# Where the last block's ssm residual stands between two ff groups, and three smaller placements, in a conditioned block kernel on Trainium2

## The chip, the cores and the metric

The kernel runs on one core of one Trainium2 chip. The metric is the device time of one execution in microseconds (us). A core has TensorE (PE; PEld is its weight load), VectorE (DVE), ScalarE (ACT), GpSimd (POOL), and SyncE (SP), which here only issues DMAs. Each engine takes its own instructions in the order in which the program issued them, and waits on semaphores for the others.

## The reference

Two sequences of 2048 tokens with 512 features pass one conditioned block. `cond` gives six modulation vectors for each sequence.

```python
emb = jnp.dot(jax.nn.silu(t), ada_w) + ada_b
shift_msa, scale_msa, gate_msa, shift_mlp, scale_mlp, gate_mlp = jnp.split(emb, 6, axis=-1)
norm = _ln(x) * (1.0 + scale_msa[:, None]) + shift_msa[:, None]
h = jax.nn.gelu(jnp.dot(norm, ssm_w1) + ssm_b1, approximate=False)
ssm_out = jnp.dot(h, ssm_w2) + ssm_b2
x = x + gate_msa[:, None] * ssm_out
norm2 = _ln(x) * (1.0 + scale_mlp[:, None]) + shift_mlp[:, None]
hf = jax.nn.gelu(jnp.dot(norm2, ff_w1) + ff_b1, approximate=True)
ff_out = jnp.dot(hf, ff_w2) + ff_b2
x = x + gate_mlp[:, None] * ff_out
```

The ssm weights are 512 x 512, ff_w1 is 512 x 1024, ff_w2 is 1024 x 512. All is fp32.

## The kernel before

**Tiles.** The 4096 tokens are eight blocks of 512 (`NBLK` = 8, four for each sequence). A block's tile `x_i` is 128 partitions x 4 x 512. All weights stay in SBUF. Each 512 x 512 product of a block is done by Strassen's method in Winograd's form: seven half-size products P1 to P7 instead of eight, with sums of quarters of both operands made ahead (`sums_of_first`, `sums_of_second`: four operations in order, which also overwrite one quarter).

**Groups.** `group` (L268) issues the seven products in the order P1, P2, P6, P5, P7, P3, P4 (in the start also FIRST, with P5 ahead of P6). A product has two halves j, and each half 2 or 4 values of k. Products accumulate in three PSUM banks: P1, P6, P7 and P4 in "y", P2 in "x", P5 and P3 in "v". Each tag has two buffers, one for each group in turn. After each product `after` reads the bank (VectorE, in P4 of hidden groups ScalarE), and then the operations hung on that product in `hooks` are issued. So the place of a hook is its place in the queues of all engines. `EARLY` is P1, P2, P6, P5, P7.

**Stages of a block i.** Names in the profile follow them:
- `hA_i`: first ssm product and gelu (`First`); `hSA` are the sums of its result.
- `oA_i`: second ssm product, added to x_i (`residual`, L469, read at L483).
- `hC_i`: first ff product, in two groups of 256 hidden columns each, `hC_i_0` and `hC_i_1` (`Second`); `hSC` are the sums of its result, `hC.summed(0)` and `hC.summed(1)`.
- `oC_i`: second ff product, added to x_i, then stored.

A norm (`Norm`) consists of `stats` (VectorE), `scales` (eight small POOL instructions, L325 to L336), `normal` (ScalarE, L349), `turn` (VectorE, 32 x 32 transposes), `move` (sixteen DMAs on SP that exchange blocks between partitions, L369), `moved` (ScalarE, modulation, L392) and `summed` (L218 to L221). In the start, `normal` is followed by TensorE transposes instead (`turned`, L378).

**The main loop (L700)**, for block i: hC_i group 0, hC_i group 1, oA_{i+1}, oC_i, hA_{i+2}. In group 1, n1 of block i+2 is scaled, normalized, turned and moved; in oA_{i+1} it is modulated, and at P3 and P4 the stats of n2 of block i+1 are taken. In oC_i that norm is scaled, normalized (P1), turned (P2, P2, P6), moved (P6) and modulated (P3), and after oC_i its sums are made on POOL. Blocks 6 and 7 have no hA_{i+2}; after oC_6, hC_7 follows at once. In the last oC_7 only P4 is `parted`: each half is read and stored for itself.

**The start.** `IDLE` = 6 matmuls on the identity come first. SP issues the loads of x_0, ada_0, ada_1, w1, ada_2, w2, x_1, ada_3, ada_4, b2's row (`b2_bc`), fw1, later ada_5 and fw2. In hA_0, `ssm_gate` multiplies b2's row with the gate (L630), folds the gate into w2 (L251, `fold2`: four folds on VectorE and four sums on POOL), and the four biases (L496) follow on POOL. Operation 7 of `fold2` is the last sum, L221. `n1[1].scales` opens the hooks of oA_0.

Of the kernel before, what the change touches and what calls it, by code (L numbers as in the profile page):

```python
# [36 lines left out]
F32 = mybir.dt.float32  # L37
# [6 lines left out]
def kernel(  # L44
# [17 lines left out]
    P = 128  # L62
# [23 lines left out]
    out_blk = out.flatten_outer_dims().rearrange("(i p c) d -> i p c d", p=P, c=C)  # L86

    G = 32
    IDLE = 6


    R_COND, R_ADA = 0, B * KD
# [8 lines left out]
    def load_x(i, pieces=1):  # L101
        xs[i] = big_tile(f"x_{i}")
        for s in range(pieces):
            c = slice(s * C // pieces, (s + 1) * C // pieces)
            nc.sync.dma_start(out=xs[i][:, c, :], in_=x_blk[i][:, c, :])
# [3 lines left out]
    def load_ada(g):  # L109
        ada[g] = big_tile(f"ada_{g}")  # L110
        nc.sync.dma_start(
            out=ada[g], in_=ada_w[:, g * D : (g + 1) * D].rearrange("(k p) n -> p k n", p=P)
        )
# [7 lines left out]
    def load_row(t, row):  # L121
        nc.sync.dma_start(out=t, in_=row.unsqueeze(0).to_broadcast([P, D]))
        return t
# [21 lines left out]
        )  # L145
    w2_sb = load_w("w2", w2)
    load_x(1)
    load_ada(3)
    load_ada(4)
    b2_bc = work.tile([P, D], F32, tag="gb", name="gb2_0", bufs=2)  # L150
    load_row(b2_bc, b2)
    fw1_sb = load_w("fw1", fw1)

    def ada_rows(g, bias=None, pa=None):
# [113 lines left out]
    def group(name, kdim, lhs, rhs, after, hooks, parted=(), order=ORDER):  # L268


        ps = {}
        for p in order:
            b = BANK[p]
            fresh = b not in ps
            if fresh:
                ps[b] = ps_g.tile([P, 2, HT], F32, tag=b, name=f"p{b}_{name}")
            for j in range(2):
                for k in range(kdim):
                    nc.tensor.matmul(  # L279
                        ps[b][:, j, :],  # L280
                        lhs(p, j, k),
                        rhs(p, j, k),
                        start=(fresh and j == 0 and k == 0),
                        stop=(p in ("P2", "P3", "P4") and k == kdim - 1),
                        skip_group_check=True,
                    )
                if p in parted:
                    after(p, ps, slice(j, j + 1))
            if p not in parted:
                after(p, ps, slice(0, 2))  # L290
            for op in hooks.get(p, ()):
                op()

    def hook(hooks, places, ops):

        for n, op in enumerate(ops):
            hooks.setdefault(places[min(n, len(places) - 1)], []).append(op)
# [171 lines left out]
    def residual(name, i, hops, wops, kdim, hooks, last=False, order=ORDER):  # L469

        xt = xs[i]
        F = D // 2
        q = {
            "11": xt[:, 0:2, :F],
            "12": xt[:, 0:2, F:],
            "21": xt[:, 2:4, :F],
            "22": xt[:, 2:4, F:],
        }
        dest = {"P1": "11", "P2": "11", "P6": "12", "P5": "22", "P7": "22", "P3": "12", "P4": "21"}

        def after(p, ps, js):
            d = q[dest[p]][:, js]
            nc.vector.tensor_tensor(d, ps[BANK[p]][:, js], d, ALU.add)  # L483
            if last and p == "P7":
                nc.sync.dma_start(out=out_blk[i][:, 2:4, F:], in_=xt[:, 2:4, F:])
            if last and p == "P4":
                s = slice(2 + js.start, 2 + js.stop)
                nc.sync.dma_start(out=out_blk[i][:, s, :F], in_=xt[:, s, :F])

        parted = ("P4",) if last else ()  # L490
        group(name, kdim, hops, lambda p, j, k: wops[p][:, k, :], after, hooks, parted, order)

    def biases(i, gb):
# [53 lines left out]
    def run(ops):  # L547
        for op in ops:
            op()
# [17 lines left out]

    idle = ps_g.tile([P, C, P], F32, tag="v", name="idle")
    for n in range(IDLE):
        if n == IDLE - 2:  # L570
            nc.tensor.transpose(pt[:, :ROWS], rows, ident[:ROWS, :ROWS])
        nc.tensor.matmul(  # L572
            idle, ident, ident.unsqueeze(1).to_broadcast([P, C, P]), start=True, stop=True
        )
# [57 lines left out]
    def fold2(lo, hi):  # L632
        return [lambda k=k: found["w2"][1][k]() for k in range(lo, hi)]
# [3 lines left out]
    st = n1[1].stats()  # L637
    hook(hooks, ("P5",), st[:1])
    hook(hooks, ("P6",), st[1:2] + [ssm_gate] + fold2(0, 2) + biases(0, b2_bc))
    hook(hooks, ("P7",), fold2(2, 8))  # L640
    hook(hooks, ("P3",), st[2:])
    hA[0] = First(0, n1[0].ops, hooks, FIRST)
    w2_ops = found["w2"][0]

    hA_sums = hA[0].summed(nc.vector)
    hooks = {}
    hook(hooks, ("P1",), [n1[1].scales] + hA_sums[:2])

    def conditioning():
        rows_3 = ada_rows(3)  # L650
# [36 lines left out]
    def fold5(lo, hi):  # L687
        return [lambda k=k: found["fw2"][1][k]() for k in range(lo, hi)]
# [11 lines left out]
    for i in range(NBLK):  # L700
        nxt, nx2, last = i + 1 < NBLK, i + 2 < NBLK, i + 1 == NBLK
        if nx2:
            n1[i + 2] = Norm(i + 2, 1)

        hooks = {} if i else first_hooks
        if nxt:
            hook(hooks, EARLY if i else ("P2",), hA[i + 1].summed(nc.gpsimd))
        if nx2:
            hook(hooks, ("P2", "P3", "P4"), n1[i + 2].stats())
        if fold:  # L710
            hook(hooks, ("P5", "P7"), fold[:2])
        hC = Second(i)
        hC.group(0, n2[i].ops, hooks)

        hooks = {}
        if nx2:
            hook(hooks, ("P1",), [n1[i + 2].scales])
            hook(hooks, EARLY, [lambda c=c: n1[i + 2].normal(c) for c in range(C)])
            hook(hooks, ("P7", "P3", "P3", "P4"), [lambda c=c: n1[i + 2].turn(c) for c in range(C)])
            hook(hooks, ("P4",), [n1[i + 2].move])  # L720
        hook(hooks, EARLY, hC.summed(0, nc.gpsimd))
        if i == 0:
            hook(hooks, ("P1", "P2", "P6", "P5"), fold5(4, 8))
            hook(hooks, ("P7",), fold5(8, 12) + [gb5_0] + biases(0, gb[5]))
        if fold:
            hook(hooks, EARLY, fold[2:6])
        hC.group(1, n2[i].ops, hooks)
        if i == 0:
            fw2_ops = found["fw2"][0]

        hooks = {}
        hook(hooks, EARLY, hC.summed(1, nc.gpsimd))
        if nxt:
            if nx2:
                hook(hooks, ("P7",), n1[i + 2].moved())
            if fold:
                hook(hooks, EARLY, fold[6:8])
                hook(hooks, ("P7",), fold[8:])
            n2[i + 1] = Norm(i + 1, 2)
            hook(hooks, ("P3", "P4"), n2[i + 1].stats())  # L740
            residual(f"oA_{i + 1}", i + 1, hA[i + 1], w2_ops, KD // 2, hooks)
        else:
            for p in EARLY:
                run(hooks.get(p, ()))
        fold = None

        hooks = {}
        if nxt:
            hook(hooks, ("P1",), [n2[i + 1].scales] + [lambda c=c: n2[i + 1].normal(c) for c in range(C)])
            hook(hooks, ("P2", "P2", "P6"), [lambda c=c: n2[i + 1].turn(c) for c in range(C)])  # L750
            hook(hooks, ("P6",), [n2[i + 1].move])
        if i + 3 < NBLK:
            hook(hooks, ("P6",), [lambda: load_x(i + 3)])
        refold2 = (i + 2) % PER_B == 0 and nx2
        if refold2:
            hook(hooks, ("P1",), [lambda: load_w("w2", w2, w2_sb)])
        if nx2:
            if refold2:
                gb[2] = gate_bias(gate[2, (i + 2) // PER_B], b2, "gb2_1")
            hook(hooks, ("P1", "P2"), n1[i + 2].summed(nc.gpsimd))  # L760
            hook(hooks, ("P2", "P6"), biases(i + 2, gb[2]))
        if nxt:
            hook(hooks, ("P3",), n2[i + 1].moved())
        hook(hooks, ("P3",), [lambda: store(i, 0)])
        residual(f"oC_{i}", i, hC, fw2_ops, KH // 2, hooks, last)
        if not last:
            store(i, 1)
        if nxt:
            run(n2[i + 1].summed(nc.gpsimd))

        refold5 = (i + 1) % PER_B == 0 and nxt
        if refold5:
            load_w("fw2", fw2, fw2_sb)
            gb[5] = gate_bias(gate[5, (i + 1) // PER_B], fb2, "gb5_1")
            fw2_ops, fold = weight_of_second(
                fw2_sb, fw2_s, gate[5, (i + 1) // PER_B], (nc.vector,)
            )
        hooks = {}
        if nxt:
            hook(hooks, EARLY, biases(i + 1, gb[5]))  # L780
        if refold2:
            w2_ops, w2_fold = weight_of_second(w2_sb, w2_s, gate[2, (i + 2) // PER_B], (nc.gpsimd,))
            hook(hooks, ALL, w2_fold)
        if nx2:
            hA[i + 2] = First(i + 2, n1[i + 2].ops, hooks)
        else:
            for p in ORDER:
                run(hooks.get(p, ()))
# [45 lines left out]
```

## Time and profile before

| what | us |
|---|---|
| runs | 626.52, 627.17, 1312.7; median 627.17 |
| the profiled execution | 626.36 |
| its span | 624.5 |
| PE busy in the span | 612.0 (98%) |
| POOL, DVE, ACT busy | 359.4 (58%), 295.1 (47%), 176.5 (28%) |
| chain that ended last, PE's share | 92% |
| mean granted TensorE clock | 0.997 |

Times within the span are counted from its first instruction. A line of a timeline has start, busy time, engine, line of the program, operation, out<-in by the program's names, shapes, count, and in brackets the engine's idle time before it with what ended it. One half-size product of a hidden group, or of oA, is eight matmul records and 1.73 us; one of oC is sixteen and 3.45. A hidden group or an oA is 12.09 us, an oC 24.17.

### The profile page before, as it was taken

How to read it: one execution, taken by the hardware profiler on the slowest of the kernel's cores; microseconds unless marked ns; L12 is line 12 of the kernel's file. 1: busy time of each engine (PE TensorE's matmuls, PEld its weight loads, DVE VectorE, ACT ScalarE, POOL GpSimd, SP SyncE). 2: the span in 40 equal slices, each digit the busy share in tenths (PEclk: the TensorE clock that was granted, in tenths of full speed). 3: DMA queues.
4: the chain of work that ended last, by engine and by line, in shares of the span. 5: the costliest groups of instructions: out<-in, count | busy, mean ns of one | idle time of the engine just before them, and what ended most of it. 6: DMA issues, size and time to landing. Idle time of an engine off the chain costs nothing.

```text
span 624.5 us, 7738 instructions
## 1 busy us (share of the span) xinstructions
PE 612.0 (98%) x2837; PEld 525.5 (84%) x2837; DVE 295.1 (47%) x491; ACT 176.5 (28%) x265; POOL 359.4 (58%) x376
## 2 busy tenths in 40 slices
PE   8999999999999999999999999999999999997997
PEld 4677888888888888888888888888888888886886
DVE  3876585434553355524553368533555233532311
ACT  2232531333320522332422333214313323012110
POOL 3396659937725745549937369958446373305430
PEclk9999999999999999999999999999999999998999
DMA  8961002050022402351021720133020400012001
GB/s 327 415 236 68 2 0 68 22 181 2 17 52 67 136 0 56 98 153 51 0 68 35 241 81 24 44 78 124 1 60 17 127 1 0 1 43 93 1 0 68
DMA packets 22057, 47.72 MB, mean 76 GB/s; under 512 B 4052, under 2 KB 4608, under 8 KB 21124
## 3 DMA queue, kind: packets, MB, share of 16 engines
q1 hardware_dynamic: 21936, 47.20, 24.0%
q8 instruction: 22, 0.36, 0.2%
q14 instruction: 15, 0.12, 0.1%
q10 hardware_dynamic: 84, 0.03, 0.0%
HBM read 25.20 MB, written 8.39 MB: 54 GB/s over the span
## 4 chain that ended last, share of the span: by engine, by line
PE 92%; POOL 3%; ACT 1%; DVE 1%; issue 1%; DMA 0%; POOLq 0%; SPq 0%
PE py_oC L279 18%; PE py_hC L279 18%; PE pv_hC L279 9%; PE pv_oC L279 9%; PE py_oA L279 8%; PE py_hA L279 8%; PE px_oC L279 4%; PE pv_oA L279 4%; PE px_hC L279 4%; PE pv_hA L279 4%; PE px_oA L279 2%; PE px_hA L279 2%; PE idle L572 1%; ACT blocks L349 1%; PE pt L378 1%
## 5 line engine op out<-in xcount | busy, mean ns | idle before, releaser
L392 ACT ACTIVATE nT<-nT,mod,mod 128x512 f32<-128x512 f32 x52 | 38.1, 802 | 173.0 <-DMA nT<-blocks 160.9
L496 POOL TENSOR_TENSOR x<-x,gb 128x512 f32<-128x512 f32 x64 | 79.8, 1280 | 10.0 <-issue 9.9
L279 PE MATMUL py_hC<-nS,fw_s 128*128 128x256 f32 x256 | 62.1, 387 | 2.2 <-POOL nS L220 2.2
L218 POOL TENSOR_TENSOR nS<-nT 128x512 f32<-128x512 f32 x13 | 16.5, 1271 | 80.7 <-ACT nT L392 58.5
L279 PE MATMUL py_oC<-fw_s,hSC 128*128 128x256 f32 x256 | 57.9, 379 | 0.0
L349 ACT ACTIVATE nT<-x,nmr,rstd 128x512 f32<-128x512 f32 x52 | 38.6, 803 | 67.1 <-POOL nmr L336 67.1
L279 PEld LDWEIGHTS py_hC<-nS,fw_s 128*128 128x128 f32 x256 | 49.4, 193 | 9.5 <-POOL nS L220 2.6
L279 PEld LDWEIGHTS py_oC<-fw_s,hSC 128*128 128x128 f32 x256 | 48.6, 190 | 6.6
L483 DVE TENSOR_TENSOR x<-py_oC,x 128x512 f32<-128x512 f32 (+1 forms) x33 | 22.2, 674 | 61.3 <-PE py_oC L279 61.3
L325 POOL TENSOR_SCALAR ve<-mv 128x4 f32<-128x4 f32 x16 | 4.3, 266 | 76.8 <-DVE mv L317 76.3
L316 DVE BATCH_NORM_STATS2 st<-x 128x6 f32<-128x512 f32 x64 | 43.2, 674 | 5.0 <-DMA x<-in_x_dram 4.7
L208 POOL TENSOR_TENSOR hSC<-hClo 128x512 f32<-128x512 f32 x16 | 20.4, 1273 | 29.4 <-ACT hClo L432 29.4
L360 DVE STREAM_TRANSPOSE blocks<-nT 128x512 f32<-128x512 f32 x52 | 34.0, 688 | 4.6 <-ACT nT L349 4.6
L483 DVE TENSOR_TENSOR x<-py_oA,x 128x512 f32<-128x512 f32 x32 | 22.1, 690 | 24.9 <-PE py_oA L279 24.3
L279 PE MATMUL py_hC<-nT,fw 128*128 128x256 f32 x128 | 30.6, 381 | 1.2 <-ACT nT L392 1.2
L279 PE MATMUL py_hA<-nS,w_s 128*128 128x256 f32 x128 | 30.3, 380 | 0.4 <-DVE u2hA L443 0.4
L279 PE MATMUL pv_hC<-nT,fw 128*128 128x256 f32 x128 | 30.4, 380 | 0.0
L279 PE MATMUL py_oA<-w_s,hSA 128*128 128x256 f32 x128 | 30.3, 380 | 0.0
L279 PE MATMUL pv_hC<-nT,fw_s 128*128 128x256 f32 x128 | 30.2, 379 | 0.0
L279 PE MATMUL py_hC<-nS,fw 128*128 128x256 f32 x128 | 30.2, 379 | 0.0
L279 PE MATMUL px_hC<-nT,fw 128*128 128x256 f32 x128 | 30.2, 379 | 0.0
L279 PE MATMUL py_oC<-fw_s,hChi 128*128 128x256 f32 x128 | 29.2, 380 | 0.5 <-DVE x L483 0.5
(146 smaller groups left out, 1251.6 us busy)
## 6 DMA issues: line engine op xcount, KB each, us to landing
nT<-blocks SPq DMA_DIRECT2D x208, 64.0 KB, 2.0
out_dram<-x SPq DMA_DIRECT2D x15, 512.0 KB, 7.5
x<-in_x_dram SPq DMA_DIRECT2D x7, 1024.0 KB, 6.9
ada<-in_L_cond_ada_w_dram SPq DMA_DIRECT2D x6, 1024.0 KB, 12.1
fw<-in_L_cond_ff_w_dram SPq DMA_DIRECT2D x3, 2048.0 KB, 15.2
w<-in_L_cond_ssm_w_dram SPq DMA_DIRECT2D x3, 1024.0 KB, 6.5
x<-in_x_dram SPq DMA_DIRECT2D x2, 512.0 KB, 4.6
gb<-in_L_cond_ssm_b_dram SPq DMA_DIRECT2D x2, 256.0 KB
```

Source lines behind the costliest of these rows:

```text
L208: lambda: eng.tensor_tensor(s[1], q["11"], q["21"], ALU.subtract),
L218: lambda: eng.tensor_tensor(s[1], q["22"], q["12"], ALU.subtract),
L279: nc.tensor.matmul(ps[b][:, j, :], lhs(p, j, k), rhs(p, j, k), start=(fresh and j == 0 and k == 0), stop=(p in ("P2", "P3", "P4") and k == ...
L316: nc.vector.bn_stats(st, xs[self.i][:, c, :])
L325: v.tensor_scalar(ve, self.mv[:, :, 1], EPS, None, ALU.add)
L349: nc.scalar.activation(t, x_c, AF.Identity, bias=self.nmr[:, c : c + 1], scale=self.rstd[:, c : c + 1])
L360: nc.vector.transpose(self.bl[:, :, :, c, :].rearrange("p m k q -> p k m q"), self.nT[:, c, :].rearrange("p (k m q) -> p k m q", k=KD, m=C),)
L378: nc.tensor.transpose(pt[:, c * P : (c + 1) * P], self.xn[:, c, k * P : (k + 1) * P], ident)
L392: nc.scalar.activation(dst, src, AF.Identity, bias=shift, scale=scale)
L483: nc.vector.tensor_tensor(d, ps[BANK[p]][:, js], d, ALU.add)
L496: lambda c=c: nc.gpsimd.tensor_tensor(xs[i][:, c, :], xs[i][:, c, :], gb, ALU.add)
L572: nc.tensor.matmul(idle, ident, ident.unsqueeze(1).to_broadcast([P, C, P]), start=True, stop=True)
```

## The change

Four edits.
1. `group` gives a parted product's bank two tiles, one for each half j, and starts each of them anew; in oC_7 now P1, P6, P7 and P4 are parted, which are all the products of bank "y". P7's quarter is stored in halves, too.
2. In block 6 (`early`), oA_7 is put between hC_6's groups 0 and 1. n2 of block 7 is then scaled, normalized, turned (P6, P6, P5, P7) and moved (P7) in group 1, modulated in P5 of oC_6, and its sums are on VectorE. `hC.summed(0)` goes with oA_7, `hC.summed(1)` into P1, P1, P1, P2 of oC_6. The loop's body is regrouped into functions for this; by that `hC.summed(0)` enters the hooks of group 1 ahead of n1's scales in blocks 0 to 5.
3. b2's row is loaded ahead of ada_3 and ada_4, and w2's last sum (operation 7 of `fold2`) is moved from P7 of hA_0 behind `n1[1].scales` in P1 of oA_0.
4. `IDLE` is 5. The transpose of `rows` still follows four idle matmuls.

```diff
-    IDLE = 6
+    IDLE = 5
...
     load_x(1)
+    b2_bc = work.tile([P, D], F32, tag="gb", name="gb2_0", bufs=2)
+    load_row(b2_bc, b2)
     load_ada(3)
     load_ada(4)
-    b2_bc = work.tile([P, D], F32, tag="gb", name="gb2_0", bufs=2)
-    load_row(b2_bc, b2)
...
+            apart = p in parted
             if fresh:
-                ps[b] = ps_g.tile([P, 2, HT], F32, tag=b, name=f"p{b}_{name}")
+                ps[b] = [
+                    ps_g.tile([P, 2, HT], F32, tag=b, name=f"p{b}_{name}_{n}") for n in range(1 + apart)
+                ]
             for j in range(2):
                 for k in range(kdim):
                     nc.tensor.matmul(
-                        ps[b][:, j, :],
+                        ps[b][j * apart][:, j, :],
                         lhs(p, j, k),
                         rhs(p, j, k),
-                        start=(fresh and j == 0 and k == 0),
+                        start=(fresh and j * (not apart) == 0 and k == 0),
...
-                if p in parted:
-                    after(p, ps, slice(j, j + 1))
-            if p not in parted:
-                after(p, ps, slice(0, 2))
+                if apart:
+                    after(p, {b: ps[b][j]}, slice(j, j + 1))
+            if not apart:
+                after(p, {b: ps[b][0]}, slice(0, 2))
...
-            if last and p == "P7":
-                nc.sync.dma_start(out=out_blk[i][:, 2:4, F:], in_=xt[:, 2:4, F:])
-            if last and p == "P4":
+            if last and p in ("P7", "P4"):
                 s = slice(2 + js.start, 2 + js.stop)
-                nc.sync.dma_start(out=out_blk[i][:, s, :F], in_=xt[:, s, :F])
-
-        parted = ("P4",) if last else ()
+                f = slice(F, D) if p == "P7" else slice(0, F)
+                nc.sync.dma_start(out=out_blk[i][:, s, f], in_=xt[:, s, f])
+
+        parted = ("P1", "P6", "P7", "P4") if last else ()
...
-        if n == IDLE - 2:
+        if n == IDLE - 1:
             nc.tensor.transpose(pt[:, :ROWS], rows, ident[:ROWS, :ROWS])
...
-    hook(hooks, ("P7",), fold2(2, 8))
+    hook(hooks, ("P7",), fold2(2, 7))
...
-    hook(hooks, ("P1",), [n1[1].scales] + hA_sums[:2])
+    hook(hooks, ("P1",), [n1[1].scales] + fold2(7, 8) + hA_sums[:2])
...
+        def second_group(hooks):
+
+            if nx2:
+                hook(hooks, ("P1",), [n1[i + 2].scales])
+                hook(hooks, EARLY, [lambda c=c: n1[i + 2].normal(c) for c in range(C)])
+                hook(hooks, ("P7", "P3", "P3", "P4"), [lambda c=c: n1[i + 2].turn(c) for c in range(C)])
+                hook(hooks, ("P4",), [n1[i + 2].move])
...
+            hC.group(1, n2[i].ops, hooks)
+
+        def ssm_residual(hooks):
+
             if nx2:
                 hook(hooks, ("P7",), n1[i + 2].moved())
...
             n2[i + 1] = Norm(i + 1, 2)
             hook(hooks, ("P3", "P4"), n2[i + 1].stats())
             residual(f"oA_{i + 1}", i + 1, hA[i + 1], w2_ops, KD // 2, hooks)
+
+        def norm_2(hooks, turns, then):
+
+            hook(hooks, ("P1",), [n2[i + 1].scales] + [lambda c=c: n2[i + 1].normal(c) for c in range(C)])
+            hook(hooks, turns, [lambda c=c: n2[i + 1].turn(c) for c in range(C)])
+            hook(hooks, (then,), [n2[i + 1].move])
+
+        early = nxt and not nx2
+        hooks = {}
+        hook(hooks, EARLY, hC.summed(0, nc.gpsimd))
+        if early:
+            ssm_residual(hooks)
+            hooks = {}
+            norm_2(hooks, ("P6", "P6", "P5", "P7"), "P7")
+        second_group(hooks)
...
+        hooks = {}
+        hook(hooks, ("P1", "P1", "P1", "P2") if early else EARLY, hC.summed(1, nc.gpsimd))
+        if nx2:
+            ssm_residual(hooks)
+            hooks = {}
+        elif not nxt:
             for p in EARLY:
                 run(hooks.get(p, ()))
+            hooks = {}
...
+        if nx2:
+            norm_2(hooks, ("P2", "P2", "P6"), "P6")
...
-            hook(hooks, ("P3",), n2[i + 1].moved())
+            hook(hooks, ("P5" if early else "P3",), n2[i + 1].moved())
...
-            run(n2[i + 1].summed(nc.gpsimd))
+            run(n2[i + 1].summed(nc.vector if early else nc.gpsimd))
```

More of the change, by code (lines that the diff above doesn't have):

```diff
@@ L713 @@
         hC.group(0, n2[i].ops, hooks)
[L715 to L733, printed above, removed]
+        def second_group(hooks):
[4 more added lines that the diff above has]
+                hook(hooks, ("P4",), [n1[i + 2].move])
+            if i == 0:
+                hook(hooks, ("P1", "P2", "P6", "P5"), fold5(4, 8))
+                hook(hooks, ("P7",), fold5(8, 12) + [gb5_0] + biases(0, gb[5]))
+            if fold:
+                hook(hooks, EARLY, fold[2:6])
+            hC.group(1, n2[i].ops, hooks)
+        def ssm_residual(hooks):
             if nx2:
@@ L741 @@
             residual(f"oA_{i + 1}", i + 1, hA[i + 1], w2_ops, KD // 2, hooks)
-        else:
+        def norm_2(hooks, turns, then):
[10 more added lines that the diff above has]
+        second_group(hooks)
+        if i == 0:
+            fw2_ops = found["fw2"][0]
+        hooks = {}
[4 more added lines that the diff above has]
+        elif not nxt:
             for p in EARLY:
                 run(hooks.get(p, ()))
+            hooks = {}
         fold = None
[L747 to L751, printed above, removed]
+        if nx2:
+            norm_2(hooks, ("P2", "P2", "P6"), "P6")
         if i + 3 < NBLK:
```

## The prediction

> **What bounds the kernel.** I read four views in this order: who waited for whom on TensorE, busy time by stretch, the timelines of all engines around each wait, and the chain of waits. The first, in total microseconds, times, longest:
>
> ```profile
> PE py_hC L279 <- POOL nS L220: 2.2, 1, 2.2
> PE py_hA L279 <- DVE s5hA L448: 1.5, 1, 1.5
> PE idle L572 <- POOL ident masks.py:199: 1.3, 1, 1.3
> PE py_hC L279 <- ACT nT L392: 1.2, 1, 1.2
> PE pt L378 <- ACT blocks L349: 1.1, 3, 0.4
> PE pmod L182 <- ACT adarows L169: 0.7, 1, 0.7
> PE py_oC L279 <- DVE x L483: 0.5, 1, 0.5
> PE py_hA L279 <- DVE u2hA L443: 0.4, 1, 0.4
> ```
>
> All of TensorE's waits come to 8.9 us. The stretches (length, then busy time of PE, PEld, DVE, ACT, POOL, granted clock, DMA) say where they lie:
>
> ```profile
> 16.69:33.54 16.85, 15.36 (x68) 11.49 (x69) 14.16 (x22) 3.81 (x6) 6.75 (x6) 1.00 1.04 414
> 68.77:566.20 497.43, 497.43 (x2302) 436.81 (x2300) 238.10 (x394) 144.80 (x216) 298.86 (x307) 1.00 0.21 59
> 566.20:573.55 7.35, 3.99 (x17) 2.88 (x17) 2.07 (x3) 3.56 (x5) 3.79 (x3) 1.00 0.32 130
> 573.55:577.00 3.45, 3.45 (x9) 2.73 (x10) 0.00 (x0) 0.00 (x0) 3.43 (x3) 0.54 0.00 0
> ```
>
> From 68.77 to 566.20 TensorE never stops: there the change can only lose. It can win in the start, at the joint between blocks 6 and 7, and at the end. The timelines give the causes:
>
> ```profile
> 29.17 0.69 DVE L630 TENSOR_TENSOR gb<-pgate,gb 128x512 f32<-128x512 f32 x1 [2.31 <-DMA gb<-in_L_cond_ssm_b_dram]
> 44.84 2.93 ACT L349 ACTIVATE blocks<-x,nmr,rstd 128x512 f32<-128x512 f32 x4 [5.16 <-POOL nmr L336]
> 554.35 10.50 SPq L369 DMA_DIRECT2D nT<-blocks  x16
> 566.54 2.93 ACT L392 ACTIVATE nT<-nT,mod,mod 128x512 f32<-128x512 f32 x4 [15.26 <-DMA nT<-blocks]
> 569.55 1.27 POOL L218 TENSOR_TENSOR nS<-nT 128x512 f32<-128x512 f32 x1 [21.23 <-DMA out_dram<-x]
> 619.19 1.99 PE L279 MATMUL py_oC<-fw_s,hChi 128*128 128x256 f32 x8 [0.52 <-DVE x L483]
> ```
>
> At the joint a chain runs late: sixteen moves leave SP until 564.85, ScalarE modulates until 569.47, POOL adds three times until 573.5. (POOL's wait is put down to a store, but ScalarE's last write ended 0.08 before it.)
>
> **What the Trainium skill says.** *TensorE: Matmul & The Clock Gate*, "What's actually happening": TensorE falls to half clock after an idle window of about 3.4 us. The trace agrees in kind: after waits of 1.2 and 2.15 us the clock is 0.54 and eight matmuls take 3.54 us, not 1.73. *SBUF — State Buffer*, "SBUF: two separate sides": a VectorE operation with two SBUF inputs and a GpSimd one exclude each other. It agrees: L219 on VectorE took 1.64 us beside POOL's w1 sums, 0.69 alone (55.03). *PSUM — Partial Sum Buffer*, "PSUM bank collisions raise a hardware error": readers and writers are kept apart by bank; hence the 0.52 us above, where j=1 waits for the reader of j=0. *DMA: Bandwidth & Descriptors*, "Queues, rings and completion order": each engine takes a ring's descriptors in order[...].
>
> **Start: IDLE 6 to 5.** It removes the last warm-up matmul, two records of 0.48 us before `pada` at 9.97: 0.96 us. ada_0 landed by 9.1 (issued 1.63, shortest landing 7.4), silu ended at 8.7. ScalarE's normals wait for nmr (11.34), not for TensorE; they end at 12.9 instead of 13.1, just when TensorE would want them. I take **0.8**; bounds 0.2 (normals decide) and 0.95.
>
> **Start: b2's row.** In the queue it passes two 1 MB loads. At the 409 GB/s of this stretch they take 2.1/0.409 = 5.1 us, so it lands near 24 instead of 29.15. x_1 is still ahead of it (issued 8.27, longest landing 13.7: 22.0; used at 24.56). ada_3 and ada_4 move back by 0.26/0.409 = 0.64 us and are used at 37; SP's three issues end at 18.9 in either order. VectorE then reaches L630 at 26.2 (26.86 less 0.65, the part of the 0.8 that gets through POOL's w1 sums), not 29.17. Behind it in VectorE's queue stood two folds (1.27) and L448, the read of bank y that P4 of hA_0 awaits: L448 ends at 28.7, TensorE gets to P4 at 29.45, and its 1.49 us wait goes, with 0.1 of a slow first matmul: **1.6**. Bounds 0.5 (row lands late) and 1.6.
>
> **Start: the weights' sum.** L221 (1.59 us) leaves the POOL queue ahead of the eight `scales` instructions of block 1 and comes behind them. POOL runs biases 4.95, three sums some 4.7, scales 3.39 from 27.0 on: nmr at about 40.0 instead of 44.81. ScalarE's four normals (2.93) end at 43 instead of 47.77, before TensorE asks at 43.6. The first transposes took 46.17 to 48.15 where their like take 0.45: **1.5**; bounds 0.8 and 1.5. w2's s[2] is needed by P4 of oA_0 near 46.2; it is ready at 41.6. Given back: fw1's four sums on POOL (9.7 us) now end at 51.3 and cover VectorE's nS sums, which start at 50.1. That slows one or two by 0.7; u2hA (L443) already ends a wait there. I take **minus 0.4**, bounds minus 1.0 and 0. Start in all **3.5**.
>
> **Second groups of blocks 0 to 5.** Here `hC.summed(0)` now enters before n1's scales, and this sits under the saturated stretch. One POOL operation, pitch 1.35 us, goes ahead of scales. In block 3 POOL has no gap (scales 304.87 to 307.94): normals start at 309.3, not 307.97. ScalarE's queue holds three gelus behind them; the last would end at 314.6, not 313.26. VectorE's turn of the last quarter ends some 0.2 us later, near 313.4; its next read of a bank is at 314.21. POOL's order past these two is unchanged, SP's moves start 0.2 later and have microseconds. Where POOL idles (block 0: scales waited 5.66 us for mv) nothing moves. I cost it at **0**; a cost would need VectorE over 0.8 us late, a gain is excluded as TensorE has no wait there. Bounds 0 and 0.5 a block.
>
> **Joint.** oA_7 (12.09 us) goes ahead of hC_6's second group; TensorE's sum is the same. oA_7's operands: hSA_7's sums end at 511.9, and it starts at 517.85. With T = end of oA_7 (529.94), read from the offsets of before:
> - Stats end at T+3.13, so L437 (bank y) ends at 3.74; P6, due at 3.45, starts at 3.8: **-0.35**. Before, the same stats lay beside a product of 3.45 us and cost nothing.
> - scales end at 6.29; normals 6.32 to 9.25. Turns 0 and 1 stand before L446 in VectorE's queue, so L446 ends at 9.1; P3, due at 8.97 plus the 0.35, wants bank v at 9.3: near nothing, **-0.15** allowed. P2's gelu waits behind the normals to 9.9; POOL needs it only after P3's gelu at 12.3.
> - Moves start at T+10.95, last 10.50 plus 1.7 to land: T+23.2. Modulation ends at T+26.1, ten microseconds before hC_7 (T+36.8). hC_6's second sums, all in P1 and P2 of oC_6, need 12.35+4 = 16.4; P6 of oC_6 comes at 19.5. SP has store(6,0) only after P3, so it isn't held.
> - nS sums of block 7 now stand on VectorE behind the last read of oC_6 and before L437 of hC_7. From its end E: read to 0.7, four sums of 0.72 to 3.5 (POOL's biases of block 7 are long done, so no lock), L437 to 4.1. P6, due at 3.45, starts at 4.2: **-0.75**. A wait of 0.75 us stays far from the clock's drop; the 1.49 us one at 30 left it at 1.00.
>
> Before, oC_6's end to hC_7's end took 30.02 us (566.20 to 596.22) for 24.17 of work: 5.85 lost. Now 1.25 are lost: **4.6**. Bounds 2.5 (another 2 us in VectorE's queue) and 5.2.
>
> **End.** Bank y's products of oC_7 go to one bank per half. P4's j=1 starts at 618.68, not 619.19, without the slow start (1.99 against 1.73): **0.75**. The six half reads of 0.42 replace three of 0.69, VectorE is idle 2.7 us before each. P7's store becomes two issues of 0.4, five microseconds before the last. Bank for j=1 is freed by hC_7's last gelu (597.1), and is wanted at 597.95. Bounds 0 and 0.8; the last store, 128 KB, stays as it is.
>
> **Sum.** 3.5 + 0 + 4.6 + 0.75 = 8.85. The profiled execution took 626.36 (span 624.5, 1.86 around it), 0.81 under the median of the runs shown. 626.36 - 8.85 = 617.5; from the median, **618.3**, 1.4% less.
>
> **Rivals.**
> 1. *VectorE becomes the bound at the joint* (chance 0.15). Its queue holds stats, turns and sums in front of bank reads. Against: the offsets above. If turns 0 and 1 held it for the whole of scales plus normals (another 3 us), the clock would fall too (1.6 as before): gain 0 at the joint, 622.9.
> 2. *The start doesn't follow* (0.15): b2 isn't what L630 waited for last, or fw1's sums give it back. Start 0.5 instead of 3.5: 621.3.
> 3. *The change of POOL's order breaks the saturated stretch* (0.07): scales behind a sum that awaits a gelu, normals late, turns late, a bank read late, in each of six blocks. It decides beyond 8.85/6 = 1.5 us a block, that is VectorE 2.3 us later than its 0.8 of slack and the 0.2 already used allow. At 3 us a block: 618.3 + 18 = 636, slower. Over 3.6 us a block it passes 2%.
>
> The main case has 0.63; its own spread is 616 to 620.5. The range 615.5 to 622.5 takes it, rival 2 and half of rival 1. Two per cent, about what a measurement of this kernel can tell from no change, is 12.5 us; all of TensorE's waits and the slow clock come to less, so faster by more gets 0.03, slower by more 0.03.
>
> **What would show it.** No wait before L630; L349's normals near 40; no wait at P4 of hA_0; full clock throughout; a wait of some 0.7 us at P6 of hC_7 released by L437, and one of 0.3 at P6 of hC_6's second group; no wait before the last eight matmuls. Any wait between 66 and 517 would prove the cost of zero wrong.

## The result and the profile after

The changed kernel takes 618.05 us (median of 6 runs, 617.91 to 623.0) against 626.64 beside it: ratio 0.9884, with a 95% interval of [0.9846, 0.9921]. (The two medians alone give 0.9863; the one run of 623.0 draws the ratio up.) A second comparison, with `e_again` below, gave 0.9871 [0.9857, 0.9886]. The forecast was 618.3. The profiled execution took 617.91, its span is 616.1. One thing is needed to read these numbers: the same kernel before takes 624.7 us in executions with a mean granted clock of 1.00 and 626 to 627 in those with 0.995 to 0.997, about half of each kind, and its profile is one of the latter.

TensorE's waits in the kernel after (total us, times, longest):

```profile
PE idle L575 <- POOL ident masks.py:199: 1.3, 1, 1.3
PE py_hC L283 <- DVE s1hC L441: 1.0, 2, 0.7
PE pmod L182 <- ACT adarows L169: 0.7, 1, 0.7
PE rowsT L574 <- DMA rows<-in_L_cond_ff_b_dram: 0.6, 1, 0.6
PE pv_oA L283 <- POOL ve L329: 0.5, 1, 0.5
PE pada L159 <- DMA ada<-in_L_cond_ada_w_dram: 0.5, 1, 0.5
PE py_hA L283 <- DVE u2hA L447: 0.4, 1, 0.4
PE pt L382 <- ACT blocks L353: 0.3, 1, 0.3
```

The two largest waits on data are gone (POOL's nS at block 7, s5hA at P4 of hA_0), as is the one before the last eight matmuls. New ones stand in their place: two of `py_hC` on VectorE's L441, one of `pv_oA`, and two on loads. These are the lines of after that answer to the timelines of before (b2's row, the normals of block 1, the modulation of block 7, the product that it feeds, and the last product):

```profile
26.18 0.67 DVE L633 TENSOR_TENSOR gb<-pgate,gb 128x512 f32<-128x512 f32 x1
40.04 2.93 ACT L353 ACTIVATE blocks<-x,nmr,rstd 128x512 f32<-128x512 f32 x4 [3.00 <-POOL nmr L340]
549.05 2.93 ACT L396 ACTIVATE nT<-nT,mod,mod 128x512 f32<-128x512 f32 x4 [8.86 <-DMA nT<-blocks]
567.64 2.00 PE L283 MATMUL py_hC<-nS,fw_s 128*128 128x256 f32 x8 [0.70 <-DVE s1hC L441]
609.18 3.62 PE L283 MATMUL py_oC<-fw_s,hChi 128*128 128x256 f32 x16
```

The stretches (length, then busy time of PE, PEld, DVE, ACT, POOL, granted clock, DMA share, GB/s) show what they cost:

```profile
65.20:514.12 448.92, 448.92 (x2078) 394.89 (x2077) 219.13 (x363) 138.10 (x205) 286.45 (x292) 1.00 0.22 63
526.21:539.14 12.93, 12.61 (x57) 10.48 (x56) 9.57 (x18) 4.71 (x7) 2.57 (x9) 1.00 0.02 5
563.32:576.38 13.06, 12.36 (x58) 10.57 (x57) 7.42 (x11) 1.89 (x3) 0.10 (x1) 1.00 0.10 40
576.38:588.46 12.08, 12.08 (x57) 10.65 (x56) 4.15 (x6) 2.73 (x5) 5.07 (x5) 1.00 0.01 1
```

The last row is a hidden group without a wait. hC_6's second group (second row) is 0.85 longer, hC_7's first (third row) 0.98. From the start of hC_0 to the end of hC_6's first group both kernels take 448.92 us (68.77 to 517.69 before): up to where the change takes another order, the saturated stretch is the same to the last digit. Set side by side, by the starts of hC_0 and of oC_7:

| stretch | before | after | gain | forecast |
|---|---|---|---|---|
| to hC_0 | 68.77 | 65.20 | 3.57 | 3.5 |
| hC_0 to oC_7 | 527.29 | 523.26 | 4.03 | 4.6 |
| oC_7 to the end | 28.44 | 27.64 | 0.80 | 0.75 |
| span | 624.5 | 616.1 | 8.40 | 8.85 |

### The profile page after: what moved, and what is told of

Its sections match the earlier page's. It is cut to its first block, busy times and chain, and to the rows that moved or that the text cites. A ratio compares the mean times of both kernels' runs of the same rounds, so it can differ in the third digit from the quotient of the medians.

```text
span 616.1 us, 7729 instructions
## 1 busy us (share of the span) xinstructions
PE 607.3 (99%) x2835; PEld 524.2 (85%) x2835; DVE 297.4 (48%) x498; ACT 176.3 (29%) x265; POOL 354.3 (58%) x372
## 4 chain that ended last, share of the span: by engine, by line
PE 93%; DVE 2%; POOL 2%; DMA 1%; ACT 1%; issue 1%; SPq 0%; DVEq 0%; POOLq 0%
PE py_oC L283 18%; PE py_hC L283 17%; PE pv_hC L283 9%; PE pv_oC L283 9%; PE py_oA L283 9%; PE py_hA L283 8%; PE pv_oA L283 5%; PE px_oC L283 4%; PE px_hC L283 4%; PE pv_hA L283 4%; PE px_oA L283 2%; PE px_hA L283 2%; DMA ada<-in_L_cond_ada_w_dram 1%; PE pt L382 1%; POOL x L499 1%
## 5 line engine op out<-in xcount | busy, mean ns | idle before, releaser
L283 PE MATMUL py_hC<-nS,fw_s 128*128 128x256 f32 x256 | 60.7, 380 | 1.0 <-DVE s1hC L441 1.0
L218 POOL TENSOR_TENSOR nS<-nT 128x512 f32<-128x512 f32 x12 | 15.3, 1272 | 59.3 <-ACT nT L396 58.3
L487 DVE TENSOR_TENSOR x<-pv_oC,x 128x512 f32<-128x512 f32 x16 | 11.1, 691 | 37.9 <-PE pv_oC L283 37.9
```

Source lines behind the costliest of these rows:

```text
L218: lambda: eng.tensor_tensor(s[1], q["22"], q["12"], ALU.subtract),
L283: nc.tensor.matmul(ps[b][j * apart][:, j, :], lhs(p, j, k), rhs(p, j, k), start=(fresh and j * (not apart) == 0 and k == 0), stop=(p in (" ...
```

## The experiments

Each measured figure is the ratio to the kernel before, run beside it, with its 95% interval in brackets; microseconds behind it are worked out from the ratio.

**The parts, each alone on the kernel before.** `e_start` takes the edits of IDLE, of b2's row and of the sum:

> Only the start's edits on the kernel before: IDLE 5, b2's row ahead of ada_3 and ada_4, w2's last sum behind the scales. My theory (three separate gains at start, joint and end that add up, as TensorE is saturated between them): 3.5 us less than before, and no wait between 66 and 566 us. The rival (early progress is given back later, at the joint with block 7, where the chain of norm and moves sets the pace): under 1 us less, with longer waits at the joint.

Measured 0.9942 [0.9923, 0.996], some 3.6 us. oA_0's first product starts at 32.53 and hC_0 at 66.31, 2.46 us earlier than before, in a profile in which the second ada product ran at half clock (1.94 us instead of 1.06). The joint is the old one, waits of 1.40 and 2.17 and a slow product:

```profile
571.32 3.48 PE L279 MATMUL py_hC<-nS,fw_s 128*128 128x256 f32 x8 [2.17 <-POOL nS L220]
```

TensorE has no wait between 66 and 566 us, and nothing is given back at the joint; the rival falls.

`e_joint` keeps the start and the end of before and takes the rest:

> Only the order of block 6 (oA_7 between the two ff groups, norm of block 7 earlier, its sums on VectorE), with the regrouped hooks; start and end as before. My theory: 4.0 to 4.6 us less; waits of some 0.3 us at P6 of hC_6's second group and 0.7 us at P6 of hC_7, both released by the first read of bank y, and full clock. The rival (VectorE becomes the bound there): under 1.5 us less, and a granted clock below 1 after hC_7's start.

Measured 0.994 [0.9924, 0.9955], 3.75 us, a little under the 4.0 that was expected, and the medians (622.44 against 625.41) give 3.0 only; why is told under "Why the prediction was right". hC_0 (68.98) to oC_7 (592.25) is 523.27 us, that of the changed kernel to 0.01. The wait at hC_7's P6 is 0.71, from L438, the line of L441. The clock of the joint is full, and four of five executions have 1.00. The fifth, which is the profiled one, has 0.996: its slow stretch lies in the start.

`e_tail` takes only the banks and the stores:

> Only the banks of the last residual split by halves, and P7's quarter stored in halves. My theory: 0.75 us less, all between the last eight matmuls and the end; no wait before them. The rival (the second y bank or the extra store costs it back): 0 to 0.2 us less, with a wait at the head of oC_7 or a later last store.

Measured 0.9994 [0.9983, 1.0004]: by the runs alone inconclusive, since the kernel's spread is wider than the effect, and only one of its 14 executions has a clock of 1.00 (623.69 us), against 14 of 27 of the kernel before (median 624.68). Why so few isn't known. The trace decides it. oC_7's start (596.52) to the end (624.2) is 27.68 against 28.44, 0.76 less, and the last sixteen matmuls run without a stop:

```profile
617.24 3.62 PE L282 MATMUL py_oC<-fw_s,hChi 128*128 128x256 f32 x16
```

`e_order` takes only the regrouped order of POOL:

```diff
         hooks = {}
+        hook(hooks, EARLY, hC.summed(0, nc.gpsimd))
         if nx2:
...
-        hook(hooks, EARLY, hC.summed(0, nc.gpsimd))
```

> Only the order of POOL in the second ff group of each block: the sums of the first group's hidden values go ahead of the next norm's scales, as the regrouping of hooks brings it. My theory: no difference (within 0.3 us), though the four normals of block 5's norm, 307.97 us before, start 1.2 to 1.35 us later. The rival (the saturated stretch is sensitive to it): 1.5 us or more per block, 9 us slower.

Measured 0.9999 [0.9986, 1.0012]. Block 5's norm is made in the second group of block 3. Its first normal starts at 309.24, 1.27 later than before, and VectorE's last turn ends at 313.43 (forecast 313.4). TensorE doesn't notice.

**How far that cover reaches.** `e_order4` hangs all four sums on P1, ahead of the scales:

```diff
+        hook(hooks, ("P1",) if nx2 else EARLY, hC.summed(0, nc.gpsimd))
         if nx2:
...
-        hook(hooks, EARLY, hC.summed(0, nc.gpsimd))
```

> The order of POOL pushed further: all four sums of the first ff group ahead of the next norm's scales, at P1, in blocks 0 to 5. My theory (the cover is VectorE's 0.8 us of slack before its first read of the next group, where POOL has no gap): scales 5.4 us later in blocks 3 and 4, turns hold VectorE, TensorE waits some 2 us in each of these two blocks and nowhere else: 3 to 4.5 us slower. The rival (order on POOL never reaches TensorE): no difference. The other rival (every block is hit): 10 us slower or more.

Measured 1.0122 [1.01, 1.0144], 7.6 us slower. The places are as forecast, blocks 3 and 4 only, the size isn't: I had 2 us in each, the profile has 2.5 and 3.5, and its span is 6.5 us longer than before. The rest of the 7.6 fits the clock: none of its five executions has 1.00, against 16 of 36 of the kernel before beside it. The first of these lines is VectorE held up in front of its reads of the banks, the others TensorE's two stops:

```profile
314.05 0.71 DVE L360 STREAM_TRANSPOSE blocks<-nT 128x512 f32<-128x512 f32 x1 [4.43 <-ACT nT L349]
318.12 1.97 PE L279 MATMUL py_oA<-w_s,hSA 128*128 128x256 f32 x8 [2.32 <-DVE x L483]
394.22 1.97 PE L279 MATMUL py_oA<-w_s,hSA 128*128 128x256 f32 x8 [3.34 <-DVE x L483]
```

Four turns and L451 stand between the late normal and the read that P6 of oA awaits. One sum ahead of the scales is free with 0.8 us to spare; four are not. The slower rival of the prediction names a real mechanism; the change stays on the near side of it.

**The start taken apart.** `e_b2`, the row alone, as in the diff of the change:

> Only b2's row loaded ahead of ada_3 and ada_4. My theory (the row was the last thing that L630 waited for, and P4 of hA_0 and the norm of block 1 hang on it): 2.2 to 2.9 us less; TensorE's 1.5 us wait at P4 of hA_0 gone, normals of block 1 near 42.4 us, a rest of the wait at the first transposes left. The rival (the sum in POOL's queue carries the start): under 1 us less.

Measured 0.9957 [0.9939, 0.9975], 2.7 us; hC_0 at 66.04, 2.73 earlier. Up to 0.6 of that isn't the row's: in this profile the first ada product starts at 9.36, not at 9.97. Between executions with a clock of 1.00 it is 2.35 (624.66 and 622.31). L630 has no wait, normals start at 42.10, and 0.4 us of the wait at the transposes is left.

`e_sum`, w2's last sum alone:

> Only w2's last sum moved behind the scales of block 1. My theory: normals start 1.6 us earlier (43.2 us), the wait at the first transposes shrinks, 1.4 us less; the wait at P4 of hA_0 stays at 1.5 us. So row and sum overlap, and their single gains come to more than the start's 3.5 us with IDLE's. The rival (b2's row carries all): 0.3 us less or nothing.

Measured 0.9995 [0.9984, 1.0005], hC_0 at 68.61, only 0.16 earlier. This expectation failed, and not in its first half: normals start at 43.48, the transposes end early, and hA_1 begins at 51.39 instead of 52.76, which is the 1.4 us. They are lost again at once (VectorE, POOL, then TensorE):

```profile
52.64 2.21 DVE L218 TENSOR_TENSOR nS<-nT 128x512 f32<-128x512 f32 x1 [1.08 <-ACT nT L392]
51.94 2.35 POOL L211 TENSOR_TENSOR fw_s<-fw,fw_s 128x1024 f32<-128x1024 f32 x1
55.62 1.99 PE L279 MATMUL pv_hA<-nT,w 128*128 128x256 f32 x8 [0.61 <-DVE nT L219]
```

fw1's sums on POOL end at 54.3 as before, since the moved sum still comes ahead of them. VectorE's nS sum comes earlier, meets the last of them and takes 2.21 us instead of 0.99, ending 0.56 after it; this fits the lock that the Trainium skill describes (*SBUF — State Buffer*, "SBUF: two separate sides"). With the row moved too, POOL's whole queue is 3 us earlier, and L218 takes 1.03.

`e_idle`, IDLE 5 alone:

> Only IDLE 5. My theory: the first ada product starts at 9.0 to 9.3 us, where its weights land, instead of 9.97 us; 0.3 to 0.8 us less, nothing of it lost before hC_0. The rival (the waits for b2's row and for the normals of block 1 absorb it, as neither depends on TensorE): 0 to 0.2 us less.

Measured 0.9997 [0.9984, 1.0009]. The first ada product starts at 9.05 instead of 9.97 and hA_0 0.94 earlier, but then VectorE waits for b2's row 0.4 longer, and TensorE's wait at P4 grows from 1.5 to 2.16:

```profile
29.10 0.69 DVE L630 TENSOR_TENSOR gb<-pgate,gb 128x512 f32<-128x512 f32 x1 [2.70 <-DMA gb<-in_L_cond_ssm_b_dram]
31.64 1.99 PE L279 MATMUL py_hA<-nS,w 128*128 128x256 f32 x8 [2.16 <-DVE s5hA L448]
```

hC_0 starts 0.08 earlier. The rival holds: alone it is absorbed.

**What is left at the joint.** `e_again` is the changed kernel, run beside two variants of it.

> The changed kernel itself, beside the two variants of it: 618.05 us as measured; its clock in each run tells whether runs near 623 us are those in which the clock fell.

It took 618.38. Its one execution with a clock under 1 (0.997) was the slowest, 618.9; none came near 623, so that question wasn't answered.

`e_sums_pool` makes block 7's operand sums on POOL, in oC_6:

```diff
+        if early:
+            hook(hooks, ("P3",), [lambda: run(n2[i + 1].summed(nc.gpsimd))])
...
-        if nxt:
-            run(n2[i + 1].summed(nc.vector if early else nc.gpsimd))
+        if nx2:
+            run(n2[i + 1].summed(nc.gpsimd))
```

> The changed kernel with block 7's four operand sums on POOL in P3 of oC_6, not on VectorE after it. My theory (the 0.70 us wait at P6 of hC_7 is the queue of four sums before the first read of bank y): the wait goes, 0.8 us less than the changed kernel, 617.2 us. The rival (P6 waits for the sums, or for something else): the wait stays, within 0.2 us of the changed kernel.

Measured 617.1, 0.985 [0.9834, 0.9867]. The sums end on POOL at 557.5, six microseconds before hC_7; its first group is back at 12.08 us. By itself this can't tell the two theories apart, since P6 reads the sums too, and the variant takes the queue away and brings the sums early. The trace of the changed kernel can:

```profile
566.29 0.69 DVE L221 TENSOR_TENSOR nS<-nT,nS 128x512 f32<-128x512 f32 x1
566.90 0.68 DVE L441 TENSOR_TENSOR s1hC<-py_hC,colsT 128x512 f32<-128x512 f32 x1
```

The last sum ends at 566.98, L441 at 567.58, and P6 starts at 567.64. So the read behind the queue came last. The sums alone would have held P6, due at 566.77, by some 0.2 us (estimated from these times).

`e_no_queue` also takes the stats and turns out of VectorE's way in block 6:

```diff
+            st = n2[i + 1].stats()
+            hook(hooks, ("P3", "P4"), st if nx2 else st[:2])
...
+            hook(hooks, ("P1",), st)
+            norm_2(hooks, ("P7", "P3", "P3", "P4"), "P4")
```

Here `st` in the last lines is `st[2:]`, the stats of quarters 2 and 3.

> As the last, and in block 6 the stats of quarters 2 and 3 come after the first read of hC_6's second group, with the turns in P7, P3, P3, P4 and the moves in P4. My theory: the 0.32 us wait at P6 and the delay of P3 go too, 1.4 to 1.7 us less than the changed kernel, 616.4 us, TensorE without a wait from 66 us to the end of oC_7. The rival (scales later by the wait for stats make the turns hold VectorE): no better than the other variant.

Measured 616.44, 0.9843 [0.9828, 0.9857]. From hC_0 to oC_7 TensorE never stops:

```profile
66.50:587.95 521.45, 521.45 (x2414) 458.29 (x2413) 247.00 (x407) 151.82 (x228) 314.45 (x320) 1.00 0.20 58
```

`e_idle6` is this with IDLE 6:

> The best variant so far (norm of block 7 out of VectorE's way) with IDLE 6 again instead of 5. What is open: whether the sixth warm-up matmul is worth its time. In two profiles with IDLE 5 the second ada product took 1.8 to 1.9 us instead of 1.06, at half clock, after short waits. My theory: the first ada product starts at 9.1 to 9.3 us either way, since its weights land then; the sixth matmul fills the wait before it, so the clock stays full; the median is the same within 0.3 us (616.2 to 616.7), and no execution has the slow second ada product. The rival (IDLE 5 gives its 0.8 us once the row comes early): 0.5 to 0.9 us slower, 617.1 us.

Measured 616.56, 0.9847 [0.9825, 0.9868], the same. My reason was half wrong: in its profile the first ada product starts at 10.10, not at 9.2, and hC_0 at 65.75 against 65.20 in the changed kernel. So the sixth matmul can cost 0.55 us. In three other profiles with IDLE 6 that product did start at 9.12 to 9.36. The other half is not shown either: all five executions had a clock of 1.00, and IDLE 5 had slower ones (two of six in `e_start`, whose old joint can drop as well), but these are few.

## Why the prediction was right

- **What bounds it.** That only the start, the joint and the end could give anything is shown by the trace: the stretch between has 448.92 us in both. The runs fit: the parts add up to 0.58 + 0.60 + 0.06 = 1.24%, each with 0.1 to 0.2 either way, against 1.16 and 1.29 together.
- **IDLE.** The 0.8 us on TensorE is right against the profile of before (0.92), in part by luck. The eight records of the first four idle matmuls took 6.60 us there, and 5.6 to 6.7 in the other profiles with IDLE 6, where the first ada product starts anywhere from 9.12 to 10.10; with IDLE 5 it is 9.00 to 9.32. So on TensorE the edit is worth from almost nothing to 1 us, by the execution. It counts only with the row moved; alone it is worth nothing, as b2's load sets L630.
- **b2's row.** The loads landed in the order of their issue, x_1 near 21.7 us and the row near 22.3 (forecast 22.0 and 24), so the row had 4 us to spare. L630 starts at 26.18 (forecast 26.2), P4 of hA_0 has no wait, oA_0 starts 2.64 us earlier (0.8 and 1.6 forecast). Alone it carries three quarters of the start.
- **The sum.** nmr was forecast at 40.0 and normals start at 40.04; the transposes don't wait. But the 1.5 us were not the sum's own: the row alone brings most of them, and the sum alone gives all of its share back at fw1's sums. The term "given back" was -0.4. Its size held in the whole change, its place didn't: 0.53 lies at P5 of oA_0, where VectorE's first two hSA sums meet POOL's w2 sums (1.55 and 1.66 us; before, only the second was slow, 0.68 and 1.65). b2's row had moved them onto each other (`e_b2` shows the same wait, 0.47); at fw1's sums L218 takes 1.03, as good as the 0.99 before.
- **The order in blocks 0 to 5.** Zero, shown by `e_order`; its limit by `e_order4`.
- **The joint.** The mechanism is right in each step: scales, normals, turns and moves lie within 0.1 us of their places, modulation ends at 552.0, eleven microseconds early, and the two waits stand at P6 of both groups, with 0.32 and 0.70 recorded. The mis-sized term is what they cost: 1.25 was forecast, 1.83 measured (0.85 and 0.98 in the stretches above). Each stop costs 0.2 to 0.3 more than its recorded wait: the first product after it takes 2.00 instead of 1.89, and the wait is counted from the last product's end, 1.89 after its start, where without a stop the next one begins after 1.73 (0.70 + 0.11 + 0.16 = 0.97). P3's small one (0.15) was as allowed. Hence 4.03 instead of 4.6.
- **The end.** 0.80 for 0.75; `e_tail` 0.76.

That the median fell on the forecast within 0.3 us owes something to luck. The prediction put all of the 5.85 us lost at the joint down to the order of the work. But part of it is the half clock of the one execution that was profiled. The joint of `e_sum` is that of before, and its profile has a clock of 1.00. The first line is from before, the second from `e_sum`:

```profile
573.55 3.54 PE L279 MATMUL py_hC<-nS,fw_s 128*128 128x256 f32 x8 [2.15 <-POOL nS L220]
573.61 1.99 PE L279 MATMUL py_hC<-nS,fw_s 128*128 128x256 f32 x8 [2.15 <-POOL nS L220]
```

The wait is the same, the product isn't slow. From hC_0 to oC_7 `e_sum` takes 525.82 us, not 527.29. So of the 4.03 us won at the joint some 1.5 are the drop of the clock, and 2.6 are what the order gives when there is no drop. Executions with a clock of 1.00 agree: `e_joint` takes 622.42 against 624.68, 2.3 less, and the changed kernel 618.05, 6.6 less, not the 8.40 between the two profiles. The forecast's base, two runs of 626.52 and 627.17, had times of the kind with the drop.

## What to carry to other kernels

Where one engine is saturated, list its waits, and cost each edit only at the wait that it removes; then look at what each moved instruction stands in front of. An instruction that leaves one queue's chain can run into another engine's work a few microseconds later, so a gain should be followed to the next stretch that is known to be unchanged, not only to the wait that it ends. Work with slack (operand sums of the next block, stats, turns) belongs on an idle engine or behind the bank reads in an in-order queue, not between the end of one group and the first read of the next, where four sums of 0.7 us cost TensorE 0.98 us here.

## What was not expected

The half clock at the joint comes in some executions only. Of the 27 of the kernel before that were run beside `e_start`, 14 had a granted clock of 1.00 and a median of 624.68; nine had 0.997 and 626.29, four had 0.995 and 627.08. The waits come from the program and are there in both kinds of profile, as shown above; the drop, 1.6 us in eight matmuls of the profile, is not certain to follow. The Trainium skill (*TensorE: Matmul & The Clock Gate*, "What's actually happening") says that the window runs free of the kernel, which would fit; no run here shows the window's place. The whole idle window of some 3.4 us of which the prediction spoke was not needed: waits of 1.20 and 2.15 us with work between them were enough, in some executions. With the long waits at the joint gone, 9 of 10 executions of the changed kernel had 0.997 or more. The tenth, 0.992 and 623.0 us, was not profiled, and what cost it 5 us stays open. A new place for the drop is the start, where short waits follow each other, two on loads and one on ScalarE, of 0.3 to 0.7 us: in `e_start` and `e_no_queue` the second ada product took 1.94 and 1.79 us instead of 1.06. In the changed kernel's profile the same three waits (0.56, 0.53, 0.71) left the clock at 1.00. And in the profile of `e_joint` it fell behind a longer wait of the old start, at P4 of hA_0, a product that took 1.99 us in before:

```profile
31.50 2.76 PE L280 MATMUL py_hA<-nS,w 128*128 128x256 f32 x8 [1.98 <-DVE s5hA L449]
```

So the prediction's remark that the 1.49 us wait at this place left the clock full holds for that execution, not as a limit.
